# Adapter and mixture-of-experts block: six batches' results are summed among the dynamic expert blocks instead of at the end

## The chip, the cores and the metric

The kernel runs on one core of one Trainium2 chip. The metric is the device time of one execution in microseconds (us). TensorE is called PE here, its weight loads PEld, VectorE is DVE, ScalarE is ACT, GpSimd is POOL and SyncE, which issues most transfers, is SP.

## The reference

For 16 batches of 256 tokens of width D = 256 the reference computes an adapter chosen per batch, and a feed-forward block with one shared MLP and the best two of eight experts per token:

```python
# adapter: weights of the batch's profile
z = relu(x @ Wd + bd)                        # 256 -> 128
y = x + z @ Wu + bu                          # 128 -> 256
h = layernorm(y) * g + b
# feed-forward on h
router_probs = softmax(h @ gate_w + gate_b)  # 8 experts
expert_values, expert_indices = top_k(router_probs, k=2)
expert_values = expert_values / (sum(expert_values) + 1e-09)
moe_out = sum over the two experts e of value_e * (gelu(h @ ew1[e] + eb1[e]) @ ew2[e] + eb2[e])
shared  = gelu(h @ sh_w1 + sh_b1) @ sh_w2 + sh_b2      # 256 -> 1024 -> 256
return x + h + shared + moe_out
```

All of it is float32. How many tokens go to which expert is known only on the chip. For these inputs the experts get 940, 931, 1119, 1065, 1411, 1083, 845 and 798 of the 8192 pairs of token and expert.

## The kernel before, in words

**Numbers.** Weights and activations of the MLPs are split into two float16 parts, and a product is three matmuls (high by high, high by low, low by high). One *unit* is 256 tokens through one MLP: eight groups of six matmuls for the first product (`mm1`, L667) and eight for the second (`mm2`, L703). After each group of the first, ACT applies gelu (L674); after every fourth, the four results are split into high and low parts: high by ACT (L682) or DVE (L684), low by DVE (L688). A *half unit* has 128 tokens. The groups of one unit's first product alternate with those of the second product of the unit before (`unit_steps`); a second product that has not yet run waits in `pend`.

**Static stage, up to about 392 us.** A planner (`Plan`) is given operations with engine, duration, dependencies and a due time, and lays them out one after the other on all engines: of the operations that can start, it takes the one with the smallest key of start, due time and load. The constants `P_V`, `PACE` and `VE2` set due times: of the expert weights' preparation and of the units that fill PE. In this stage lie the adapter (L823, L839, L843), the transposes (L958), the gate (L977), the ranks of each token within its experts (L1047 to L1054), the scatter of each token's row into the experts' slots `xslot` in DRAM (L1092), 13 of the 16 shared units, the preparation of each expert's weights (squares on ACT at L533, high parts on ACT at L616, low parts on DVE at L622), the table of blocks, and the first 14 expert units. Each expert has two *static* blocks of 256 slots. Tokens of rank 512 and above belong to blocks whose expert is found on the chip.

**Dynamic stage, units s = 14 to 36.** Two static units are left (14, 15), then sixteen dynamic full units (16, 17, 18, 20 to 22, 24 to 26, 28 to 30, 32 to 34, 36) with half units between them (19, 23, 27, 31, 35). Here SP's and POOL's orders are as written in the code; PE, DVE and ACT are ordered by the framework's scheduler. In each unit SP issues the transposing loads of the rows of unit s+2 and their row numbers (`next_T`: L1227 and L1231, twice for a full unit), then its weights if the expert changes (`block_weights`: L1544, L1546), then for s = 19 to 34 one batch of x again (`x_again`, L1635). DVE takes a finished result from PSUM with its weights' scale and the bias (`take`, L1234), POOL scatters it to `yrow` in DRAM, where each token has two rows (`scatter_y`, L1240), and adds x and the shared bias into `base` for one batch (`add_x`, L1640, L1641).

**Weights of the two experts.** `top2_weights`, called in the loop at s = 18, takes Exp of the logits (L1580) and some thirteen small DVE operations; the scheduler puts it at 184 us, since it depends on the routing only.

**End.** The number of used blocks is read (L1672) and a branch (L1673) runs further half units if there are more than five; for these inputs there are not. Then shared unit 13 (`whole_unit`), eight loads of 1 MB of `yrow` into the buffers of the weights and of the adapter's result (`combine_load`, L1604), shared units 14 and 15, and for each of 16 batches `combine` and `store`. `combine` adds two rows times two weights into `base`: four operations on DVE (L1619) or, for even batches, two on DVE, two scales on ACT (L1617) and one add on POOL (L1624). Shared results are added into `base` by DVE (L1503).

## Time and profile before

| what | value |
|---|---|
| median of three runs | 665.37 us |
| lowest and highest | 664.24 and 669.65 us |
| the profiled execution | 666.21 us, span 664.4 us, granted clock 0.960 |
| PE busy | 614.1 us, 92% of the span |
| DVE, ACT, POOL busy | 410.4, 392.4, 242.1 us |
| chain that ended last | PE 75%, DVE 8%, DMA 6%, issue 5%, ACT 3% |
| moved by DMA | 131.57 MB |

The span is what the profiler sees from the first to the last instruction; the execution's own time is 1.8 us longer. A stretch of the profile gives, for each engine, the busy time and the number of instructions in it, the TensorE clock that was granted, and the share of time that the 16 DMA engines were busy. In a group of instructions the numbers behind the bar are busy time and mean duration, and behind the next bar the engine's idle time before them with what ended it. "PEq" and the like are the engines' sequencers; "issue" is time in which an engine waited for nothing that the profile shows.

### The profile page before, as it was taken

Reading aid. Unit: us, or ns where it says so; the run is one execution under the profiler, and the core shown is the slowest. Engines: PE = TensorE matmul, PEld = TensorE weight load, DVE = VectorE, ACT = ScalarE, POOL = GpSimd, SP = SyncE. Lnnn points to the kernel's source line nnn. Section 1 sums busy time; section 2 is a strip of 40 time slices with the busy share of each in tenths; the row PEclk is TensorE's granted clock in tenths of the full one; section 3 lists DMA queues with packets and bytes.
Section 4 is the critical chain, followed back from the end, with each engine's and each line's share of the span. In section 5 each row is a group of like instructions: output and inputs, shape, how many; then the busy total and the mean of one; then the engine's idle time right before and its main releaser. Section 6 shows DMA issues by size and latency. Waiting matters only on the chain.

```text
span 664.4 us, 15240 instructions
## 1 busy us (share of the span) xinstructions
PE 614.1 (92%) x5541; PEld 522.8 (79%) x5541; DVE 410.4 (62%) x980; ACT 392.4 (59%) x615; POOL 242.1 (36%) x370
## 2 busy tenths in 40 slices
PE   4699997999998899999999999999999999997962
PEld 3368785877887688888888888898989989896851
DVE  5678786988884263567665744444555546552498
ACT  1378575696794487888988744444444545442570
POOL 1003463356368201323212222333654655561132
PEclk8579998999999899999999999999999999998997
DMA  7784545925522249498799559828996599910496
GB/s 264 249 266 131 177 152 176 343 98 206 185 75 88 73 151 178 128 255 255 205 250 292 176 136 361 204 72 229 306 231 193 153 317 171 333 58 6 171 387 219
DMA packets 92570, 131.57 MB, mean 198 GB/s; under 512 B 53548, under 2 KB 69958, under 8 KB 84551
## 3 DMA queue, kind: packets, MB, share of 16 engines
q1 hardware_dynamic: 84914, 109.94, 56.9%
q0 software_dynamic: 6768, 18.43, 8.4%
q10 hardware_dynamic: 804, 2.16, 0.9%
q8 instruction: 45, 0.74, 0.5%
q14 instruction: 39, 0.31, 0.1%
HBM read 96.46 MB, written 41.28 MB: 207 GB/s over the span
## 4 chain that ended last, share of the span: by engine, by line
PE 75%; DVE 8%; DMA 6%; issue 5%; ACT 3%; POOL 1%; SPq 0%; DVEq 0%; POOLq 0%; ACTq 0%
PE bank L667 35%; PE bank L703 32%; DVE base L1619 4%; DMA yrow<-late,idt 3%; PE bank L839 3%; PE bank L823 3%; DMA wst<-in_adp_dram 1%; PE bank L958 1%; DVE hh L688 1%; PE bank L843 1%; ACT h L674 1%; PE bank L977 1%; DMA wst<-yrow 1%; DMA xslot<-late,sli 1%; ACT wst L616 1%
## 5 line engine op out<-in xcount | busy, mean ns | idle before, releaser
L703 PEld LDWEIGHTS <-hh 128*128 128x128 f16 x2424 | 234.1, 99 | 47.0 <-DVE hh L688 9.6
L674 ACT ACTIVATE h<-bank,tst 128x256 f32<-128x256 f32 x256 | 139.7, 561 | 120.8 <-PE bank L667 103.3
L703 PE MATMUL bank<-wst,hh 128*128 128x256 f16 x1536 | 208.9, 273 | 1.2 <-DVEq L1673 0.9
L667 PE MATMUL bank<-late,wst 128*128 128x256 f16 x1536 | 203.8, 273 | 0.8 <-ACT h L674 0.7
L1240 POOL DMA_INDIRECT yrow<-late,idt x69 | 90.0, 1304 | 256.0 <-DVE late L1234 195.6
L667 PEld LDWEIGHTS <-wst 128*128 128x128 f16 x1536 | 150.3, 98 | 18.5 <-issue 1.1
L703 PE MATMUL bank<-wsh,hh 128*128 128x256 f16 x768 | 107.8, 278 | 12.1 <-DVE hh L688 7.0
L667 PE MATMUL bank<-xlnT,wsh 128*128 128x256 f16 x768 | 108.3, 280 | 6.9 <-PEq L1673 3.1
L674 ACT ACTIVATE h<-bank,tsh 128x256 f32<-128x256 f32 x128 | 68.9, 559 | 65.7 <-PE bank L667 57.0
L684 DVE TENSOR_SCALAR hh<-h,tst 128x1024 f16<-128x1024 f32 x46 | 41.8, 909 | 92.7 <-ACT h L674 92.6
L667 PEld LDWEIGHTS <-wsh 128*128 128x128 f16 x768 | 75.7, 101 | 23.0 <-issue 10.6
L688 DVE SCALAR_TENSOR_TENSOR hh<-h,tst,hh 128x1024 f16<-128x1024 f32 x64 | 82.0, 1281 | 17.0 <-ACT hh L682 16.0
L1092 POOL DMA_INDIRECT xslot<-late,sli x64 | 69.8, 1091 | 50.6 <-issue 23.8
L688 DVE SCALAR_TENSOR_TENSOR hh<-h,tsh,hh 128x1024 f16<-128x1024 f32 x32 | 40.9, 1278 | 34.8 <-ACT hh L682 34.4
L1234 DVE SCALAR_TENSOR_TENSOR late<-bank,tst 128x256 f32<-128x256 f32 x64 | 30.7, 480 | 36.8 <-PE bank L703 30.8
L682 ACT ACTIVATE hh<-h,tsh 128x1024 f16<-128x1024 f32 x32 | 36.7, 1147 | 0.8
L1081 POOL IOTA late<- 128x32 int32 x32 | 4.8, 160 | 74.7 <-PE bank L958 40.6
L674 ACT ACTIVATE h<-bank,late 128x128 f32<-128x128 f32 x40 | 18.3, 457 | 20.8 <-PE bank L667 19.2
L622 DVE SCALAR_TENSOR_TENSOR wst<-wf,prep,wst 128x1024 f16<-128x1024 f32 x20 | 25.3, 1279 | 0.1
L839 PE MATMUL bank<-wst,zT 128*128 128x256 f32 x64 | 23.2, 447 | 0.3
L823 PE MATMUL bank<-xlnT,wst 128*128 128x256 f32 x64 | 20.4, 449 | 2.9 <-DMA wst<-in_adp_dram 2.8
L616 ACT ACTIVATE wst<-wf,prep 128x1024 f16<-128x1024 f32 x20 | 21.3, 1136 | 1.8 <-DVE prep L578 1.8
(225 smaller groups left out, 587.8 us busy)
## 6 DMA issues: line engine op xcount, KB each, us to landing
wst<-scr SPq DMA_DIRECT2D x32, 1024.0 KB
scr<-wst SPq DMA_DIRECT2D x16, 1024.0 KB
wf<-scr SPq DMA_DIRECT2D x10, 1024.0 KB
wst<-yrow SPq DMA_DIRECT2D x6, 1024.0 KB
wf<-in_ew_dram SPq DMA_DIRECT2D x5, 1028.0 KB
wf<-in_ew_dram SPq DMA_DIRECT2D x5, 1024.0 KB
wst<-in_adp_dram SPq DMA_DIRECT2D x16, 256.5 KB
xlnT<-in_xT_dram SPq DMA_DIRECT2D x16, 256.0 KB
```

The lines of the kernel that those rows point to most:

```text
L616: ACT.activation(self.w[:, a:b], self.wf[h][:, f], AF.Copy, scale=sc[:, 2 * h : 2 * h + 1],)
L667: mm = PE.matmul(pa[:, 0:n_tok], w1[:, wl, c, k, :], xin[:, xl, k, 0:n_tok], start=i == 0, stop=i == len(seq) - 1,)
L674: ACT.activation(h32[:, c % 4, 0:n_tok], pa[:, 0:n_tok], AF.Gelu_apprx_tanh, bias=tail[:, c : c + 1], scale=tail[:, 8:9],)
L682: ACT.activation(hi, h4, AF.Copy, scale=tail[:, 9:10])
L684: V.tensor_scalar(hi, h4, tail[:, 9:10], None, ALU.mult)
L688: V.scalar_tensor_tensor(hh[:, 1, c, 0:n_tok], h32[:, :, 0:n_tok], tail[:, 9:10], hh[:, 0, c, 0:n_tok], ALU.mult, ALU.subtract,)
L703: PE.matmul(py, hh[:, hl, k, t * P : (t + 1) * P], w2[:, wl, k, :], start=q == 0 and i == 0, stop=q == 3 and i == len(seq) - 1,)
L823: PE.matmul(pt_of(("z", b))[:, 0:S], wa()[:, k * P : (k + 1) * P], xf32(b)[:, k, :], start=k == 0, stop=k == KC - 1,)
L839: PE.matmul(pt_of(("y", b))[:, t * D : (t + 1) * D], zT()[:, t * P : (t + 1) * P], wa()[:, 256:512], start=True, stop=False,)
L1092: ins = POOL.indirect_dma_start(out=xslot[:, :], out_offset=bass.IndirectOffsetOnAxis(ap=sli[:, c, j : j + 1], axis=0), in_=payb[plan.slot ...
L1234: V.scalar_tensor_tensor(ysb, py, tail[:, 10:11], tail[:, 11 : 11 + D], ALU.mult, ALU.add)
L1240: ins = POOL.indirect_dma_start(out=yrow[:, :], out_offset=bass.IndirectOffsetOnAxis(ap=idt[:, t, :].bitcast(I32), axis=0), in_=ysb, in_of ...
```

## The change

1. `top2_weights` becomes part of the plan: its operations are given to the planner after the static units, and its first depends on the routing and on the result of static unit 11. The weights get one array, `wts`, and for the first six batches a second one, `wlate`, holds the weights of rows whose rank in their expert is 512 or more; in `wts` these are zero.
2. Six transfers write zeros to the rows of `yrow` that belong to the first six batches, in the planned stage.
3. The table gets a second count of tokens per expert, over the first six batches only, and `used` a second column: the number of used blocks, plus 64 if any of these counts is above 512.
4. In the dynamic loop, at the end of units 21 to 26, SP issues `y_load` of one of the batches 0 to 5 (512 KB); one unit later the batch is combined and stored. There are two buffers for these loads, in the adapter result's array.
5. `settle(9)` ahead of the branch goes; shared unit 13 is put ahead of it. The branch reads both columns, and is taken if the second is above the sure number; then the late rows of the six batches would be loaded, added and stored again. With these inputs the largest count of the first six batches is 475.
6. At the end five loads of 1 MB bring the other ten batches, which are combined and stored as before.
7. `P_V`, `PACE` and `VE2` get other values.

```diff
--- before.py
+++ after.py
@@ -34,6 +34,8 @@
 NHALF = 24
 SURE = 5
 TOP_AT = 18
+EARLY = 6
+EARLY_AT = TOP_AT + 3
 POS_F = 2 * NSTAT * E
 POS_H = POS_F + 2 * NFULL
 NPOS = POS_H + NHALF
@@ -145,9 +147,9 @@
         return out
 
 
-P_V = (82.0, 121.0)
-PACE = (0.0, 9.6, 24.7, 16.4)
-VE2 = 8.9
+P_V = (131.0, 214.35)
+PACE = (0.0, 8.17, 16.14, 17.464)
+VE2 = 11.504
 
 
 @with_exitstack
@@ -355,7 +357,7 @@
 
     metaf = const([1, 2, NFULL], I32, "metaf")
     metah = const([1, NHALF], I32, "metah")
-    used = const([P, 1], I32, "used")
+    used = const([P, 2], I32, "used")
     rowt = const([1, NPOS], I32, "rowt")
     PAD = NULLB
     pos = const([P, 1], F32, "pos")
@@ -1119,9 +1121,13 @@
             return const(shape, dt, "bt_" + name)
 
         pc = lambda: pt_of("count")[:, 0:E]
+        pc2 = lambda: pt_of("count")[:, E : 2 * E]
         cnt = plan.op(
             "PE", 0.2,
-            lambda: PE.matmul(pc(), ones, mc[:, NG, :], start=True, stop=True), 0.0,
+            lambda: (
+                PE.matmul(pc(), ones, mc[:, NG, :], start=True, stop=True),
+                PE.matmul(pc2(), ones, mc[:, EARLY // 2, :], start=True, stop=True),
+            ), 0.0,
             [mc_of[NG - 1]], acq=[("pt", "count")], lat=0.2,
         )
         nh, nhf = rt([P, E], I32, "nh"), rt([P, E], F32, "nhf")
@@ -1132,6 +1138,7 @@
         odd0, starts = rt([P, 1], F32, "odd0"), rt([P, 2, E], F32, "starts")
         sel, row = rt([P, 2, E], F32, "sel"), rt([P, 1], F32, "row")
         ei, prev = rt([1, P], I32, "ei"), rt([1, NFULL], I32, "prev")
+        over = rt([P, 1], F32, "over")
 
         pad = plan.op(
             "DVE", 0.1, lambda: V.tensor_tensor(padi, pc(), padbase, ALU.add), 0.0, [cnt]
@@ -1150,6 +1157,7 @@
 
             pads.append(plan.op("POOL", 1.36, pad_scatter, A(NB) + 2, [pad, *last], land=P * PW * 2))
         fns = [
+            lambda: V.tensor_reduce(over, pc2(), AX.X, ALU.max),
             lambda: V.tensor_scalar(nh, pc(), float(P - 1), None, ALU.add),
             lambda: V.tensor_scalar(nh, nh, 7, None, ALU.logical_shift_right),
             lambda: V.tensor_copy(nhf, nh),
@@ -1209,7 +1217,9 @@
                 V.memset(prev[:, i : i + 1], E - 3 + r)
             V.tensor_tensor(metaf[:, 1, :], metaf[:, 0, :], prev, ALU.not_equal)
             V.tensor_scalar(metah, ei[:, POS_H:NPOS], E - 1, None, ALU.min)
-            V.tensor_copy(used, ends[:, 1, E - 1 : E])
+            V.tensor_scalar(over, over, float(NSTAT * BLK), 64.0, ALU.is_gt, ALU.mult)
+            V.tensor_copy(used[:, 0:1], ends[:, 1, E - 1 : E])
+            V.tensor_scalar(used[:, 1:2], over, ends[:, 1, E - 1 : E], None, ALU.add)
 
         plan.op("DVE", 1.0, meta, 300.0, [got])
         plan.op("DVE", 0.1, lambda: V.memset(spot, 0.0), 0.0, [got, o], add=["pa", "py0", "py1"])
@@ -1398,6 +1408,53 @@
         for s in range(NSTAT * e, min(NSTAT * e + NSTAT, NPLAN)):
             static_unit(s)
 
+
+
+    wts = const([P, 2, NTILE], F32, "wts")
+    wlate = const([P, 2, 2 * EARLY], F32, "wlate")
+
+    def top2_weights(v):
+        T8 = [P, NTILE, E]
+        rs, den = const([P, NTILE], F32, "rs"), const([P, NTILE], F32, "den")
+        rk, beyond = const([P, 2, 2 * EARLY], I32, "rk"), const([P, 2, 2 * EARLY], F32, "beyond")
+        tmp, ex = [z.rearrange("p (j e) -> p j e", e=E) for z in ztb]
+        o = plan.op(
+            "DVE", 0.4,
+            lambda: V.tensor_tensor(tmp, L, m1.unsqueeze(2).broadcast_to(T8), ALU.subtract),
+            v, [*gate_of.values(), sli_of[NG - 1], *ydone.values(), ev_last[NPLAN - 3]],
+        )
+        o = plan.op("ACT", 3.0, lambda: ACT.activation(ex, tmp, AF.Exp), v, [o])
+        fns = [lambda: V.tensor_reduce(rs, ex, AX.X, ALU.add), lambda: V.reciprocal(rs, rs)]
+        for c in range(2):
+            fns += [
+                lambda c=c: V.tensor_tensor(tmp, ex, oh[:, c], ALU.mult),
+                lambda c=c: V.tensor_reduce(wts[:, c, :], tmp, AX.X, ALU.add),
+                lambda c=c: V.tensor_tensor(wts[:, c, :], wts[:, c, :], rs, ALU.mult),
+            ]
+        e2 = slice(0, 2 * EARLY)
+        fns += [
+            lambda: V.tensor_tensor(den, wts[:, 0, :], wts[:, 1, :], ALU.add),
+            lambda: V.tensor_scalar(den, den, 1e-9, None, ALU.add),
+            lambda: V.reciprocal(den, den),
+            lambda: V.tensor_tensor(
+                wts, wts, den.unsqueeze(1).broadcast_to([P, 2, NTILE]), ALU.mult
+            ),
+            lambda: V.tensor_scalar(rk, sli[:, :, e2], EBLK * P - 1, None, ALU.bitwise_and),
+            lambda: V.tensor_scalar(beyond, rk, float(NSTAT * BLK), None, ALU.is_ge),
+            lambda: V.tensor_tensor(wlate, wts[:, :, e2], beyond, ALU.mult),
+            lambda: V.tensor_tensor(wts[:, :, e2], wts[:, :, e2], wlate, ALU.subtract),
+        ]
+        return tiny(fns, v, [o], dur=0.22, first=0.4)
+
+    top2_weights(0.0)
+    for b in range(EARLY):
+        plan.op(
+            "SP", 0.5,
+            lambda b=b: SP.dma_start(
+                yrow[2 * b * S : 2 * (b + 1) * S, :].rearrange("(p k) d -> p k d", p=P),
+                padrow[:, 0 : 2 * D].bitcast(F32).unsqueeze(1).broadcast_to([P, 4, D]),
+            ), 60.0 + 12 * b, after=[z_of[b + 8]], land=P * 4096,
+        )
     ahead_T = {}
     for s in (NPLAN, NPLAN + 1):
         u = units[s]
@@ -1565,63 +1622,30 @@
             g2(c)
         settle(9)
 
-    w1t = const([P, NTILE], F32, "w1t")
-    w2t = const([P, NTILE], F32, "w2t")
-    cp = ctx.enter_context(tc.tile_pool(name="cp", bufs=1))
-
-    def top2_weights():
-        T8 = [P, NTILE, E]
-
-        def rt(shape, name):
-            return cp.tile(shape, F32, tag=name, name=name)
-
-        tmp, ex = [z.rearrange("p (j e) -> p j e", e=E) for z in ztb]
-        V.tensor_tensor(tmp, L, m1.unsqueeze(2).broadcast_to(T8), ALU.subtract)
-        ACT.activation(ex, tmp, AF.Exp)
-        rs = rt([P, NTILE], "rs")
-        V.tensor_reduce(rs, ex, AX.X, ALU.add)
-        V.reciprocal(rs, rs)
-        pv = rt([P, 2, NTILE], "pv")
-        for c in range(2):
-            V.tensor_tensor(tmp, ex, oh[:, c], ALU.mult)
-            V.tensor_reduce(pv[:, c, :], tmp, AX.X, ALU.add)
-            V.tensor_tensor(pv[:, c, :], pv[:, c, :], rs, ALU.mult)
-        den = rt([P, NTILE], "den")
-        V.tensor_tensor(den, pv[:, 0, :], pv[:, 1, :], ALU.add)
-        V.tensor_scalar(den, den, 1e-9, None, ALU.add)
-        V.reciprocal(den, den)
-        V.tensor_tensor(w1t, pv[:, 0, :], den, ALU.mult)
-        V.tensor_tensor(w2t, pv[:, 1, :], den, ALU.mult)
-
-    def combine_load(g):
-        if g < NBUF:
-            yl = wst[g]
-        else:
-            yl = xlnT[:, 0:8].rearrange("p b l k s -> p (b l k s)")
-        yl = yl.bitcast(F32).rearrange("p (j c d) -> p j c d", c=2, d=D)
-        for h in range(2):
-            r0 = 2 * (g * TG + h * TG // 2)
-            SP.dma_start(
-                yl[:, 4 * h : 4 * h + 4].rearrange("p j c d -> p j (c d)"),
-                yrow[r0 : r0 + TG, :].rearrange("(j p c) d -> p j (c d)", p=P, c=2),
-            )
+    def y_load(yl, t0, nt):
+        SP.dma_start(
+            yl.rearrange("p j c d -> p j (c d)"),
+            yrow[2 * P * t0 : 2 * P * (t0 + nt), :].rearrange("(j p c) d -> p j (c d)", p=P, c=2),
+        )
         return yl
 
-    def combine(b, yl):
-        j0 = 2 * b % (TG // P)
+    def y_view(flat, nt):
+        return flat.bitcast(F32).rearrange("p (j c d) -> p j c d", c=2, d=D)[:, 0:nt]
+
+    def combine(b, yl, w=wts, lean=False):
         for t in range(2):
             j = 2 * b + t
-            for c, w in ((0, w1t), (1, w2t)):
-                y = yl[:, j0 + t, c, :]
-                if c == 1 and b in POOLED:
-                    ACT.activation(y, y, AF.Copy, scale=w[:, j : j + 1])
+            for c in range(2):
+                y = yl[:, t, c, :]
+                if c == 1 and b in POOLED and not lean:
+                    ACT.activation(y, y, AF.Copy, scale=w[:, c, j : j + 1])
                 else:
                     V.scalar_tensor_tensor(
-                        base[:, j, :], y, w[:, j : j + 1], base[:, j, :], ALU.mult, ALU.add
+                        base[:, j, :], y, w[:, c, j : j + 1], base[:, j, :], ALU.mult, ALU.add
                     )
-        if b in POOLED:
+        if b in POOLED and not lean:
             bb = base[:, 2 * b : 2 * b + 2, :]
-            POOL.tensor_tensor(bb, bb, yl[:, j0 : j0 + 2, 1, :], ALU.add)
+            POOL.tensor_tensor(bb, bb, yl[:, :, 1, :], ALU.add)
 
     def store(b):
         SP.dma_start(
@@ -1647,8 +1671,11 @@
     u = units[NPLAN - 1]
     u["ids"] = idb[plan.slot["id", NPLAN - 1]]
     ET = mybir.EngineType
+    flat = xlnT.rearrange("p b l k s -> p (b l k s)")
+    early_buf = [y_view(flat[:, o * 1024 : (o + 2) * 1024], 2) for o in (4, 6)]
     with tc.manual_schedule(engines={ET.SP, ET.Pool}):
         xr = None
+        early = {}
         pend.append((g2_steps(hhb[hh_turn], views(u["w"])[1], evac_of(u), 2), 2))
         for s in range(NPLAN, NU):
             u = units[s]
@@ -1659,31 +1686,46 @@
                 block_weights(units[s + 2])
             if s in HLOAD:
                 block_weights(HLOAD[s])
-            if s == TOP_AT:
-                top2_weights()
             if xr is not None:
                 add_x(s - TOP_AT - 2, xr)
                 xr = None
             if TOP_AT < s <= TOP_AT + NB:
                 xr = x_again(s - TOP_AT - 1)
+            b = s - EARLY_AT - 1
+            if b in early:
+                combine(b, early[b])
+                store(b)
+            b = s - EARLY_AT
+            if 0 <= b < EARLY:
+                early[b] = y_load(early_buf[b % 2], 2 * b, 2)
         if xr is not None:
             add_x(NB - 1, xr)
-        settle(9)
-        count = nc.values_load(used[0:1, 0:1], min_val=0, max_val=2 * NFULL + NHALF)
-        with tc.If(count > 2 * NFULL + SURE):
-            for j in range(SURE, SURE + 2):
-                extra_half(j)
-            with tc.If(count > 2 * NFULL + SURE + 2):
-                for j in range(SURE + 2, NHALF):
+        whole_unit()
+        most = 2 * NFULL + NHALF
+        count = nc.values_load(used[0:1, 0:1], min_val=0, max_val=most)
+        any_left = nc.values_load(used[0:1, 1:2], min_val=0, max_val=most + 64)
+        with tc.If(any_left > 2 * NFULL + SURE):
+            with tc.If(count > 2 * NFULL + SURE):
+                for j in range(SURE, SURE + 2):
                     extra_half(j)
-        whole_unit()
-        yl = {g: combine_load(g) for g in range(NT // TG)}
+                with tc.If(count > 2 * NFULL + SURE + 2):
+                    for j in range(SURE + 2, NHALF):
+                        extra_half(j)
+            for b in range(EARLY):
+                combine(b, y_load(early_buf[b % 2], 2 * b, 2), wlate, lean=True)
+                store(b)
+        yl = {}
+        for i, b in enumerate(range(EARLY, NB, 2)):
+            space = flat[:, 0:8192] if i < 2 else wst[(i - 2) // 2]
+            h = i % 2 * 4096
+            v = y_load(y_view(space[:, h : h + 4096], 4), 2 * b, 4)
+            yl[b], yl[b + 1] = v[:, 0:2], v[:, 2:4]
         for _ in fillers:
             pass
-        for b in range(NB - 1):
-            combine(b, yl[b * S // TG])
+        for b in range(EARLY, NB - 1):
+            combine(b, yl[b])
             store(b)
-        combine(NB - 1, yl[NT // TG - 1])
+        combine(NB - 1, yl[NB - 1])
         flush()
         store(NB - 1)
 
```

## The prediction

> **What bounds the kernel now.** I read the busy time by stretch first, then the chain that ended last, then the queue of SyncE (SP). Columns: stretch, its length, busy time of PE, PEld, DVE, ACT, POOL (with counts), granted clock, DMA share, GB/s.
>
> ```profile
> core 0: us, PE busy (x) PEld busy (x) DVE busy (x) ACT busy (x) POOL busy (x), PEclk, DMA share, GB/s
> 99.70:116.30 16.60, 13.19 (x83) 8.88 (x83) 10.07 (x34) 8.72 (x13) 5.25 (x12) 0.90 0.53 175
> 182.00:232.00 50.00, 43.99 (x389) 35.41 (x388) 24.21 (x101) 31.40 (x47) 28.93 (x52) 0.97 0.23 76
> 232.00:598.00 366.00, 364.77 (x3460) 327.69 (x3458) 204.03 (x287) 222.24 (x361) 134.87 (x163) 1.00 0.78 212
> 598.00:664.40 66.40, 44.35 (x365) 36.52 (x362) 42.10 (x67) 27.83 (x50) 15.09 (x15) 0.88 0.55 196
> ```
>
> PE sets the time from 232 to 598 us (1.23 us idle). So only three things can move the end: 22.1 us of idle PE in the tail, about 9.4 us in the two earlier stretches (3.4 and 6.0), and any stall put into the full middle. The tail, from the chain, PE's timeline and SP's:
>
> ```profile
> 607.93 1.44 PE L667 MATMUL bank<-xlnT,wsh 128*128 128x256 f16 x6 [3.14 <-PEq L1673]
> 618.79 3.94 DMA yrow<-late,idt
> 622.75 5.09 DMA wst<-yrow
> 650.69 9.42 DVE base L1619 x17
> 622.75 7.09 SPq L1604 DMA_DIRECT2D wst<-yrow  x6
> ```
>
> The branch costs PE 3.14 us; the last scatter lands 3.94 us after its issue, the first 1 MB load 5.09 us after that; then VectorE (DVE) combines without a pause until 661.2 and the store ends the span at 664.4, 3.2 us later. PE's last matmul is at 653.3. The tail is bound by a late start and by 16 batches of combining.
>
> **Tail: what is removed.** Six of 16 combines leave it, and shared unit 13 goes ahead of the branch. In the instruction order PE now has 220 matmuls behind the branch instead of 312. Groups of six take 0.655 us in the chain, so one matmul is 0.109 us. Before the branch PE starts the last dynamic unit's second product at 600.9 and has 116 matmuls from there: 12.7, so 613.6. (Interleaving the shared unit also covers the 0.91 us that PE waited on DVE there.) The branch costs 3.1 to 3.6 again: 617. Then 24.0 of matmuls and about 1 of slow clock: PE could end at 642.
>
> The loads wait for the last scatter. Its product ends after 96 of those matmuls, 611.4; take and scatter issue add 0.8, landing 3.94, POOL's join with the branch 0.85 (its semaphore instruction at L1673): loads at about 617, first data at 622 by the 5.09 row. The DVE rows of this tail:
>
> ```profile
> L1619 DVE SCALAR_TENSOR_TENSOR base<-wst,w1t,base 128x256 f32<-128x256 f32 x24 | 16.1, 717 | 3.0 <-DMA wst<-yrow 3.0
> L1624 POOL TENSOR_TENSOR base<-base,wst 128x512 f32<-128x512 f32 x6 | 8.1, 1350 | 24.7 <-DVE base L1619 11.6 <-ACT h L674 9.6 <-DMA out_dram<-base 3.6
> ```
>
> DVE runs from 628.3 to 661.2. Of these 32.9 us four splits L688 take 1.2 each in the chain, six L1503 0.4 each and pauses 1.5; the remaining 24.2 are eight pairs of batches, 3.0 a pair. With five pairs and the rest unchanged: 15.1 + 4.8 + 2.4 + 1.5 = 23.8, from 622 to 645.8. The last split stands behind the combines in DVE's order; 24 matmuls (2.6), one take (0.5) and the store (3.2) follow: about 652.1 against 664.4. **Tail: −12**; bounds −18 (the end set by PE: 642 and the same store and take) and −8 (data 4 us later: one more landing of a scatter in the way).
>
> **Dynamic stage: what is added.** Each of six batches adds to SP a load of 512 KB (y_load) at the end of unit b+21 and a store of 256 KB one unit later; to DVE four or two L1619 operations at 0.47; to ScalarE (ACT) two scales at 0.50 for even batches; to POOL one add at 1.35. The engine work, 1.9 us a unit, lies beside PE: from 232 to 598 DVE is busy 56%, ACT 61%, POOL 37%. What matters are waits on in-order queues. SP, POOL and the DMA share before:
>
> ```profile
> 463.98 1.23 SPq L1227 DMA_TRANSPOSE late<-xslot  x1
> 470.53 2.07 SPq L1546 DMA_DIRECT2D wst<-scr  x2
> 474.46 1.25 SPq L1227 DMA_TRANSPOSE late<-xslot  x1
> 481.23 1.38 SPq L1546 DMA_DIRECT2D wst<-scr  x2
> 466.07 1.77 POOL L1240 DMA_INDIRECT yrow<-late,idt  x1 [2.17 <-DVE late L1234]
> 479.69 1.35 POOL L1641 TENSOR_TENSOR base<-base,sb_b 128x512 f32<-128x512 f32 x1
> 454.00:480.00 26.00, 26.00 (x257) 23.48 (x255) 13.89 (x17) 11.43 (x22) 14.53 (x15) 1.00 1.07 319
> ```
>
> The reader sees two transposes with weights behind them (units 24 and 25, which PE begins at 483.0 and 491), unit 20's second scatter, a POOL add, and a DMA that is already full. Batch 0's load cannot go before that scatter has landed: 466.07 + 3.94 = 470.0. Unit 24's transpose stood at 463.98 and is queued behind it, so its weights go at about 477.5 instead of 470.5; landing in 5.09 they meet 483.0 just in time. The slack of some 7 us is spent. Then store 0 waits for POOL's new add, which follows the add ending at 481.04: 482.4. Batch 1's load goes at 482.9, unit 25's transpose at 484, its weights at 491 instead of 481.2 and land at 496 where PE wants them at 491: a stall of 3 to 5, say 4. DVE has the combine in the middle of a unit, ahead of its next splits, and waits there for the load to land; the scatters of that unit wait for the same landing. Half units (23, 27) are shortest: 2 to 6 us of DVE wait each, of which I let 1.25 reach PE in each of four units: 5. Later weights (unit 30): 1. **Dynamic stage: +10.** A 512 KB load's landing isn't in the trace: the 256 KB store's 3.2 from below, 1 MB's 5.09 from above; I take 5.09, since the stretch is full. Bounds: +3 (landing 3.2, only the stall of unit 25) and +19 (each of four waits costs PE 3.5).
>
> The Trainium skill, "SBUF — State Buffer", section "The DMA setup-cost knee", fits 2 us plus bytes at 436 GB/s to one transfer. An estimate from it is 3.2 us for 512 KB and 4.4 for 1 MB, where this trace has 5.09 for 1 MB; by it the stage would cost nearer +5 than +10.
>
> The same page, section "SBUF: two separate sides", says that a DVE operation with two SBUF inputs and a GpSimd operation that reads SBUF exclude each other for the whole instruction. The trace agrees: L1619 takes 0.47 alone and up to 1.49 beside POOL's 1.35. It speaks against putting combines among POOL's adds: up to 1.0 us more on each of two operations a unit. By the row that is 2 us a unit of DVE, beside 44% idle; by the rule, if each falls on a split that PE waits for, 6 units × 2 = 12 more.
>
> **Static stage: what is moved.** The weights' softmax leaves the routing stage for the planner, behind static unit 11, and new constants of pace reorder preparation and routing.
>
> ```profile
> 184.56 1.28 ACT L1580 ACT_TABLE_LOAD   x1
> 185.86 0.42 ACT L1580 ACTIVATE zT<-zT 128x256 f32<-128x256 f32 x1
> ```
>
> This Exp and the load back to gelu (1.28 at 187.33) are 2.98 us of ACT on the chain there. Behind unit 11 they lie where ACT has 39% idle; with that cover gone they would cost the same 3. Thirteen small DVE operations move along, four new ones come: 17 × 0.2 = 3.4 us, under DVE's idle 44%. Preparation of expert 0 (an ACT piece of 4.26 us at 101.43) now comes after most routing and no longer cuts into it. Of the 9.4 us idle I credit the 3.0 of Exp and about half of the remaining 6.4: **−6**. Bounds −12 (that and clock lost in these stretches) and +6 (routing, pulled tighter, starves PE twice as much as now). Six zero writes of 512 KB cost SP six issues of about 0.5 where the DMA share is 0.57: 0 to +1. The table's second count matmul and three more small DVE operations add less than 1 us beside the routing.
>
> **Sum.** −12 + 10 − 6 = −8. The profiled execution took 666.21 with a span of 664.4, and lies 0.84 above the median of 665.37; −8 from the median gives **657.4**. Within 1% (658.7 to 672.0) is what a measurement here can hardly tell from no change.
>
> **Rivals.**
> 1. *Early batches hidden.* Loads land in 3.2, stalls stay at +3: −12 + 3 − 6 = −15, **650**. For it: weights asked for two units ahead and 44% idle DVE. Against it: the slack of 7 us that one late scatter uses up.
> 2. *The wait moves.* The tail's gain returns as stalls of +19: −12 + 19 − 6 = +1, **666.4**. For it: SP is one queue with the transposes behind each y_load, and already waited 24.2 us for PE at L1227. Against: those waits are slack.
> 3. *DMA becomes the bound* (slower). Places: units 21 to 28, share 1.07 already. Six times 768 KB is 4.6 MB, at some 288 GB/s 16 us of a full DMA; with the waits' +10 that is +26: −12 + 26 − 6 = +8, **673.4**. It decides once the stage costs more than 12 + 6 + 6.7 = 24.7. Against it: from 506 to 598 the share is 0.72, so part of the debt is repaid.
> 4. *Routing starves* (slower): static +6 instead of −6, with 14 in the dynamic stage: −12 + 14 + 6 = +8, **673.4**. Against it: PE is idle least where shared units fill in, and they still do.
> 5. *The branch is taken*, and six batches are combined again: at least 6 × 3 = 18 us more. Counting the inputs' routes, no expert has more than 475 tokens in the first six batches, below the 512 of two static blocks. Excluded.
>
> **Chances.** Forecast 0.38 (own range 651 to 663: 0.27 faster, 0.11 within 1%); rival 1 0.21; rival 2 0.17; rival 3 0.18; rival 4 0.06. So faster 0.48, same 0.28, slower 0.24. The range of 643 to 675 takes in rivals 1 to 4 and leaves out most of their outer bounds: 0.05 below, 0.14 above.
>
> **What would show it.** Right: behind the branch some 24 us of matmuls, five 1 MB loads and ten combines, the end about 35 us behind their issue; first stalls of PE in the dynamic stage at units 25 to 28, released by weights or DVE's split; the stretch 182 to 232 with under 3 us of idle PE. Wrong: a dynamic stage without idle PE (then 650), a DMA share near 1 through unit 30 with PE waiting for transposes (then 673), or a routing stage that ends later than 232.

## The result, and the profile after

The changed kernel takes 698.15 us (median of four runs, 692.7 to 703.38) where the kernel before takes 664.81 beside it: a ratio of 1.046, with a 95% interval of 1.037 to 1.055. The forecast was 657.4, faster; it is slower by 33 us.

Two anchors split both traces into three parts: the first gelu of unit 14 and that of unit 36. The execution profiled first, 703.38 us, is the slowest of the four, so the lines below are of a second profile of the same kernel (run after_again), on a chip where the kernel before takes 645.38 us and this one 676.07, a ratio of 1.047 (1.042 to 1.051).

| part | before | first profile after | second profile after | forecast |
|---|---|---|---|---|
| start to unit 14 (static) | 388.3 | 399.5 | 371.4 | −6 |
| unit 14 to unit 36 (dynamic) | 205.7 | 237.1 | 238.7 | +10 |
| unit 36 to the end (tail) | 70.4 | 65.0 | 65.6 | −12 |

The static part differs from chip to chip; the other two hardly do. The kernel before was not profiled on the second chip. An estimate from its time there is 645.4 − 1.8 − 205.7 − 70.4 = 367.5 us for its static part, against 370.0 for the changed kernel by the same sum (676.1 − 1.8 − 238.7 − 65.6) and 371.4 in its profile: the change costs 2 to 4 us there. On the first chip the other three spans (690.9 to 696.5) less 238 and 65 leave 388 to 393, that is 0 to +5. The loss is in the dynamic stage: +31 to +33.

The busy times by stretch, second profile: units 14 to 21, units 22 to 30, units 31 to 35, tail. The second block is the whole dynamic stage of the kernel before.

```profile
core 0: us, PE busy (x) PEld busy (x) DVE busy (x) ACT busy (x) POOL busy (x), PEclk, DMA share, GB/s
371.40:448.70 77.30, 77.30 (x734) 69.55 (x733) 35.55 (x46) 35.19 (x64) 23.59 (x31) 1.00 0.74 210
448.70:565.10 116.40, 93.83 (x819) 79.30 (x817) 55.33 (x71) 39.92 (x79) 54.79 (x53) 0.91 0.67 206
565.10:610.10 45.00, 45.00 (x459) 40.85 (x457) 26.17 (x31) 20.91 (x41) 26.16 (x28) 1.00 0.81 215
610.10:675.70 65.60, 49.05 (x401) 40.65 (x399) 33.08 (x51) 27.58 (x48) 15.39 (x14) 0.92 0.37 130
```

```profile
388.30:594.00 205.70, 205.70 (x2004) 185.76 (x2002) 107.59 (x127) 94.76 (x177) 95.51 (x108) 1.00 0.80 220
```

Ahead of unit 22 and after unit 30 PE is as full as before. Between them, where the six batches are loaded, summed and stored, it is idle for 22.6 us, and its granted clock is 0.91 over 116.4 us, worth about 10 us more: together the 33 us. The DMA share of 0.67 says that the DMA engines are not full on the mean of this stretch. Who waited in this stretch (total, times, longest):

```profile
DVE base L1643 <- DMA xlnT<-yrow: 39.2, 6, 9.6
POOL yrow L1250 <- DVE late L1244: 37.3, 12, 11.1
ACT xlnT L1641 <- DMA xlnT<-yrow: 24.2, 3, 11.1
...
ACT h L676 <- DVE hh L690: 13.1, 3, 6.4
...
PE bank L669 <- ACT h L676: 8.6, 3, 5.4
...
PE bank L705 <- DVE hh L686: 6.0, 3, 3.9
...
PE bank L669 <- DMA wst<-scr: 5.4, 3, 2.5
...
PE bank L705 <- DVE hh L690: 2.5, 3, 1.2
```

And on SP's queue, before the early loads (L1626) and the stores (L1651):

```profile
SPq L1626 <- DMA yrow<-late,idt: 22.0, 4, 9.7
SPq L1651 <- POOL spot L1249: 16.4, 3, 7.5
```

DVE stands in every one of the six combines (L1643) for its load, and ACT in the scales (L1641) of the three even batches. POOL's scatters wait for DVE's takes (L1244), which stand behind the combines. PE then waits 17.1 us for gelu and splits that are queued behind combines, and 5.4 us for weights. One turn of it, from the timeline:

```profile
461.69 1.00 POOL L1250 DMA_INDIRECT yrow<-late,idt  x1 [7.79 <-DVE hh L686]
...
462.99 1.20 POOL L1250 DMA_INDIRECT yrow<-late,idt  x1 [0.19 <-DVE hh L690]
...
466.80 1.27 POOL L1648 TENSOR_TENSOR base<-base,xlnT 128x512 f32<-128x512 f32 x1
...
468.09 0.40 SPq L1651 DMA_DIRECT2D out_dram<-base  x1
...
470.51 0.37 SPq L1626 DMA_DIRECT2D xlnT<-yrow  x1
...
471.68 1.22 SPq L1237 DMA_TRANSPOSE late<-xslot  x1
...
474.96 1.67 DVE L1643 SCALAR_TENSOR_TENSOR base<-xlnT,wts,base 128x256 f32<-128x256 f32 x4 [9.63 <-DMA xlnT<-yrow]
...
475.70 1.01 POOL L1250 DMA_INDIRECT yrow<-late,idt  x1 [7.60 <-DMA late<-xslot]
...
477.08 0.39 PE L705 MATMUL bank<-wf,hh 128*128 128x256 f16 x2 [3.94 <-DVE hh L686]
...
478.30 1.35 SPq L1603 DMA_DIRECT2D wst<-scr  x2
...
484.52 1.46 PE L669 MATMUL bank<-late,wst 128*128 128x256 f16 x6 [2.54 <-DMA wst<-scr]
```

Read it downwards. Two scatters; POOL's add for batch 0 behind them; the store that waits for the add; batch 1's load behind the store and the landing of the second scatter, 7.5 us after its issue; DVE stands 9.63 us for that load; the next scatter goes out only after the load has landed (the profile puts its wait down to a transposing load issued behind that load); PE stands 3.94 us for the split behind the combine. The transposes (471.68) and weights (478.30) behind the load are late too, and PE waits for the weights at 484.52. It is a ring: load, combine, split, product, result, scatter, store, load.

The tail is shorter by 5 us, not 12. PE's timeline behind the branch:

```profile
634.90 1.44 PE L669 MATMUL bank<-xlnT,wsh 128*128 128x256 f16 x6 [3.89 <-PEq L1707]
636.13 1.48 PE L705 MATMUL bank<-wsh,hh 128*128 128x256 f16 x6
637.41 1.00 PE L669 MATMUL bank<-xlnT,wsh 128*128 128x256 f16 x6
638.25 0.27 PE L705 MATMUL bank<-wsh,hh 128*128 128x256 f16 x1
642.10 1.22 PE L705 MATMUL bank<-wsh,hh 128*128 128x256 f16 x5 [3.58 <-issue]
643.12 4.04 PE L669 MATMUL bank<-xlnT,wsh 128*128 128x256 f16 x18
```

Nineteen matmuls after the branch PE stops for 3.58 us with nothing to wait for, in the middle of a group of six, and the 18 behind that group take 4.04 us. DVE's first combine starts with the first data, and then DVE stands for a split that needs PE's products:

```profile
638.75 1.67 DVE L1643 SCALAR_TENSOR_TENSOR base<-xlnT,wts,base 128x256 f32<-128x256 f32 x4 [8.62 <-DMA xlnT<-yrow]
648.02 1.28 DVE L690 SCALAR_TENSOR_TENSOR hh<-h,tsh,hh 128x1024 f16<-128x1024 f32 x1 [7.60 <-ACT hh L684]
```

### The profile page after: what moved, and what is told of

Its sections match the earlier page's. It is cut to its first block, busy times and chain, and to the rows that moved or that the text cites. A ratio compares the mean times of both kernels' runs of the same rounds, so it can differ in the third digit from the quotient of the medians.

```text
span 701.6 us, 15276 instructions
## 1 busy us (share of the span) xinstructions
PE 627.7 (89%) x5542; PEld 531.0 (76%) x5542; DVE 412.7 (59%) x987; ACT 389.1 (55%) x614; POOL 246.6 (35%) x370
## 5 line engine op out<-in xcount | busy, mean ns | idle before, releaser
L705 PEld LDWEIGHTS <-hh 128*128 128x128 f16 x2424 | 238.2, 100 | 63.3 <-DVE hh L690 13.5
L669 PE MATMUL bank<-late,wst 128*128 128x256 f16 x1536 | 208.0, 276 | 8.7 <-DMA wst<-scr 5.0
L1250 POOL DMA_INDIRECT yrow<-late,idt x69 | 85.9, 1245 | 279.1 <-DVE late L1244 241.6
L705 PE MATMUL bank<-wsh,hh 128*128 128x256 f16 x768 | 112.6, 287 | 16.6 <-DVE hh L690 6.6
L690 DVE SCALAR_TENSOR_TENSOR hh<-h,tst,hh 128x1024 f16<-128x1024 f32 x64 | 86.6, 1353 | 19.3 <-ACT hh L684 18.5
L1094 POOL DMA_INDIRECT xslot<-late,sli x64 | 71.8, 1122 | 72.5 <-issue 33.8
L669 PEld LDWEIGHTS <-wsh 128*128 128x128 f16 x768 | 77.5, 103 | 21.5 <-issue 8.5
L1643 DVE SCALAR_TENSOR_TENSOR base<-xlnT,wts,base 128x256 f32<-128x256 f32 x30 | 14.7, 540 | 47.3 <-DMA xlnT<-yrow 47.3
L1244 DVE SCALAR_TENSOR_TENSOR late<-bank,tst 128x256 f32<-128x256 f32 x64 | 30.4, 478 | 18.3 <-PE bank L705 16.6
L669 PE MATMUL bank<-late,wf 128*128 128x128 f16 x240 | 20.6, 224 | 5.5 <-ACT h L676 5.5
L1324 DVE SCALAR_TENSOR_TENSOR base<-bank,tsh,base 128x256 f32<-128x256 f32 x26 | 12.5, 481 | 20.4 <-PE bank L705 12.6
```

The lines of the kernel that those rows point to most:

```text
L669: mm = PE.matmul(pa[:, 0:n_tok], w1[:, wl, c, k, :], xin[:, xl, k, 0:n_tok], start=i == 0, stop=i == len(seq) - 1,)
L690: V.scalar_tensor_tensor(hh[:, 1, c, 0:n_tok], h32[:, :, 0:n_tok], tail[:, 9:10], hh[:, 0, c, 0:n_tok], ALU.mult, ALU.subtract,)
L705: PE.matmul(py, hh[:, hl, k, t * P : (t + 1) * P], w2[:, wl, k, :], start=q == 0 and i == 0, stop=q == 3 and i == len(seq) - 1,)
L1094: ins = POOL.indirect_dma_start(out=xslot[:, :], out_offset=bass.IndirectOffsetOnAxis(ap=sli[:, c, j : j + 1], axis=0), in_=payb[plan.slot ...
L1244: V.scalar_tensor_tensor(ysb, py, tail[:, 10:11], tail[:, 11 : 11 + D], ALU.mult, ALU.add)
L1250: ins = POOL.indirect_dma_start(out=yrow[:, :], out_offset=bass.IndirectOffsetOnAxis(ap=idt[:, t, :].bitcast(I32), axis=0), in_=ysb, in_of ...
```

## The experiments

Ratios are to the kernel before, run beside each kernel on the same chip. "Stage" is the dynamic part, from the profile, 205.7 us before.

**Static stage.** Edits: the three constants of before put into the changed kernel (old_pace), the three new ones into the kernel before (new_pace).

```diff
-P_V = (82.0, 121.0)
-PACE = (0.0, 9.6, 24.7, 16.4)
-VE2 = 8.9
+P_V = (131.0, 214.35)
+PACE = (0.0, 8.17, 16.14, 17.464)
+VE2 = 11.504
```

> The changed kernel with the three constants of before (P_V, PACE, VE2). Theory S, the new order of the static stage costs what the traces show (unit 14 begins at 399.5 us instead of 388.3): about 11 us less than the changed kernel's 698, so 687, and unit 14 begins near 388. Rival T, the planned softmax and the zero writes cost it, not the constants: unit 14 stays near 399 and the time near 698. Both leave the dynamic stage (units 14 to 36) at about 237 us, against 205.7 before.

> The kernel before with the three new constants alone. Theory S: unit 14 begins about 11 us later, 676 in all. Rival T: unit 14 near 388 and 665. By the prediction's own term for the reordering it would be faster, about 661.

old_pace: 1.052 (1.045 to 1.060), unit 14 at 404.6 us, stage 238.7. new_pace: 1.0125 (1.007 to 1.018), unit 14 at 403.1, stage 206.0. On the same chip unit 14 is at 396.1 with the constants and softmax of before (run shared_ahead) and at 392.9 with the new constants and the planned softmax (run load_first). So each half alone costs 7 to 8.5 us in these profiles (one of each), and both together cost nothing there (−3): theory S fails for the pair, and T as well. The new constants belong to the planned softmax; that the two together gain over the kernel before is not shown.

**Shared unit ahead of the branch, alone.**

```diff
-        settle(9)
+        whole_unit()
         count = nc.values_load(used[0:1, 0:1], ...)
...
-        whole_unit()
         yl = {g: combine_load(g) for g in range(NT // TG)}
```

> The kernel before with shared unit 13 put ahead of the branch alone. By the prediction's tail the loads of results are issued at about 617 instead of 622.75 us and DVE combines all 16 batches without a pause after them: 5 to 6 us less, about 659.5. Rival: the branch costs more with the two units' work piled up ahead of it (5.3 us of idle PE in the changed kernel, 3.1 before), and what is gained ahead of it is lost again: 663 to 665.

Ratio 1.0007 (0.998 to 1.003), tail 72.3 against 70.4: the expected 5 to 6 us did not come. PE's timeline there:

```profile
626.24 1.44 PE L667 MATMUL bank<-xlnT,wsh 128*128 128x256 f16 x6 [3.53 <-PEq L1673]
...
632.83 0.80 PE L703 MATMUL bank<-wsh,hh 128*128 128x256 f16 x3 [2.70 <-issue]
633.42 3.42 PE L667 MATMUL bank<-xlnT,wsh 128*128 128x256 f16 x18
```

The branch costs 3.53, about as before (3.14), but the same pause without a cause follows, 2.70 us, with slow matmuls behind it. In the kernel before, where the result loads start nearly 15 us after PE has passed the branch, there is none. So the rival came true, nothing gained; but the branch itself grew by 0.4 us only, and the pause is the larger part of what is lost.

**Load at the unit's start.** The `y_load` block moved from the end of the loop's body ahead of `unit_steps`.

> The changed kernel with each y_load issued at the start of its unit instead of its end, so that it waits for a scatter one unit older. Theory W, the dynamic stage's extra 31 us are the loop from a scatter's landing through y_load, DVE's combine, the splits behind it and the next scatter: the DVE waits for the loads (38.8 us) nearly vanish, the stage falls by 15 to 25 us, to 675 to 683. Rival B, the DMA engines' bytes are what is short (share near 1, 4.6 MB more): the stage keeps at least 25 of its 31 us, 692 or more.

Ratio 1.0445 (1.037 to 1.052), stage 245.9: a clear miss. In the code's order the last scatter ahead of the start of unit s is that of unit s−2, and the load waits for it all the same, now ahead of both transposes: the first load goes out at 467.05 us, 8 us after PE has begun unit 21. The framework put the combine earlier too. DVE still stands 37.8 us at its loads. The experiment did not remove the wait that it was to remove.

**The changed kernel again, and parts left out.**

```diff
 # resident, no_load
+    resident = [y_view(flat[:, o * 1024 : (o + 2) * 1024], 2) for o in (8, 10)]
-                combine(b, early[b])
+                combine(b, resident[b % 2])
 # no_load, in addition
-                early[b] = y_load(early_buf[b % 2], 2 * b, 2)
+                early[b] = None
 # loads_only
-            if b in early:
-                combine(b, early[b])
-                store(b)
```

> The changed kernel unchanged, beside the runs below on their chip: ratio near 1.046 to the kernel before. The dynamic stage, from the first gelu of unit 14 to that of unit 36, is expected to be 235 to 240 us again (205.7 before) if its loss belongs to the order of the work; if it was an accident of one execution it is below 225.

> The changed kernel, but the early combines read two buffers that nothing loads, while the six loads are still issued as they were (the six batches' expert sums are left out of the result). Theory W, the in-order waits of DVE and ACT for the landing of the loads: PE's stalls released by splits and gelu go, the dynamic stage falls from about 237 to 215 or less, the time by 20 or more against the changed kernel. Rival Q, SP's queue: the load's wait for the scatter and the store's wait for POOL hold back transposes and weights behind them: the stage stays above 225, with PE waiting for wst<-scr. Rival B, bytes: also above 225.

> As the run with resident buffers, and the six early loads aren't issued either (the six batches' expert sums are left out); combines and stores stay. What it gains beyond that run is the price of the loads on SP's queue and on the DMA engines. Theory W: at most 5 us more, stage 206 to 215. Rival Q: the load's half of it, 10 to 15 more; what stays above 206 belongs to the stores.

> The changed kernel with its six early loads, but without the six combines and stores (the six batches are left out of the result). Theory W: nobody waits for the loads but SP and the scatters behind them, so the stage is 206 to 215. Rival Q: the load's wait alone holds SP up by 7 us a unit as the prediction had for batch 0, 215 to 225. Rival B: the bytes are there still, above 220.

Stages 238.7, 227.5, 219.8 and 225.5; ratios 1.047, 1.034, 1.020 and 1.0235 (intervals within 0.006 of these). Taking away the wait for the loads gives back 11 us, not 20; the loads alone, with nobody summing, cost 20; combines and stores without any load cost 14. Theory W missed in all three runs. Q held for the first, missed loads_only by half a microsecond, and expected 10 to 15 us between resident and no_load where there are 8. B held in the two runs for which it gave a number, so these runs don't exclude it; the plain loads below do. In loads_only PE's waits in the stretch of the early loads (440 to 565 us) are one line:

```profile
PE bank L669 <- DMA wst<-scr: 13.5, 3, 7.4
```

Every part of the early work stalls PE by itself, and by different ways. The loads do it through SP's queue, where they wait 26.3 us for scatters. In no_load PE waits 6.0 us for weights, which stand behind stores that wait 17.1 us for POOL, and 3.9 us for gelu; the combines there wait 25.0 us for POOL.

**Order on DVE and ACT, order on SP, both; and the loads of the tail held back.**

```diff
 # by_hand, behind_T_hand
-    with tc.manual_schedule(engines={ET.SP, ET.Pool}):
+    with tc.manual_schedule(engines={ET.SP, ET.Pool, ET.DVE, ET.Activation}):
...  (the tail keeps the former order)
 # behind_T, behind_T_hand: at n == 6, behind next_T, for units 21 to 28
+                    if units[s + 2]["nt"] == 2:
+                        block_weights(units[s + 2])
+                    if b >= 2:
+                        store(b - 2)
+                    if b < EARLY:
+                        early[b] = y_load(early_buf[b % 2], 2 * b, 2)
 # hold_loads
         yl = {}
+        next(fillers)
+        SP.dma_start(pos, h32b[st["h"]][:, 0, 0:1])
```

> The changed kernel with DVE's and ACT's order in the dynamic loop as written in the code, so that a combine stands behind its unit's splits and takes instead of in the middle of it; SP's order as it was. Theory W (a third of the loss, 11 of 33 us, as the run with resident buffers shows): stage 225 to 230 instead of 238.7, PE still waits for wst<-scr. If the rest were W too, 215 or less. If the place in DVE's order does not matter, 236 to 240. Units 14 to 21, which have no combine, are the control: 10.5 us a full unit.

> The changed kernel with SP's order altered in the loop: the transposes and the weights of unit s+2 are issued first, then a store of two units before, then y_load; combine as it was. Theory Q, two thirds of the loss are transposes and weights held up behind y_load's wait for a scatter and the store's wait for POOL: PE's waits for wst<-scr go and the stage falls to 215 to 222. If DVE's waits alone make the loss, it stays above 232.

> Both edits, SP's order and DVE's and ACT's. Theories W and Q together: stage 206 to 212, close to the 205.7 of before, and a ratio near 1.00 to 1.01 to the kernel before, since the tail is some 5 us shorter and the static stage some 4 longer. Theory B (bytes) would keep it above 218.

> The changed kernel with the five loads at the end held back until the first gelu after the branch, by one small transfer that reads its result. Theory F, the 3.6 us in which PE stands 19 matmuls behind the branch with nothing to wait for are the fetch of its next instructions behind the loads' bytes: the pause falls below 1 us, and the tail (unit 36 to the end) from 65.6 to about 61, though the loads come some 3.5 us later. Rival: the pause belongs to the branch and stays; tail 65 to 69.

Stages: by_hand 235.3, behind_T 229.5, behind_T_hand 225.9. All three are above what theories W and Q said, and the last lies where B would have kept it; two orders together give back 13 of 33 us of the stage. Ratios: by_hand 1.033 (1.028 to 1.039), behind_T_hand 1.032 (1.026 to 1.0385); behind_T has medians of 690.26 and 665.40 without an interval. In behind_T_hand ACT still stands 11.1 us at one load, the scatters wait 14.6 us for early loads, and the stores wait 19.3 us for POOL (16.4 in the changed kernel); only the loads' wait for scatters fell, from 22.0 to 6.8.

hold_loads did what theory F says. Its ratio, 1.041 (1.033 to 1.048), does not stand clear of the changed kernel's 1.046, but in the profile the tail is 62.2 instead of 65.6, and PE runs through:

```profile
656.07 1.44 PE L669 MATMUL bank<-xlnT,wsh 128*128 128x256 f16 x6 [3.79 <-PEq L1707]
...
659.47 0.82 PE L705 MATMUL bank<-wsh,hh 128*128 128x256 f16 x6
660.13 2.13 PE L669 MATMUL bank<-xlnT,wsh 128*128 128x256 f16 x18
```

The pause is gone though the loads come later, and 18 matmuls take 2.13 us instead of 4.04. The trace's packets on the instruction queue agree: the second 16 KB packet behind the branch starts 3.2 us after the first in hold_loads (653.46 and 656.64), 3.3 us in the kernel before, 7.0 in shared_ahead and 7.6 in the changed kernel, where 1 MB loads were issued in between. The other profiles say the same: the pause is there, 1.8 to 3.6 us after 18 to 21 matmuls, in all 16 profiles in which the loads are issued at the branch, and in none of the four in which they are issued later. That the packet's lateness is queueing behind the loads' bytes is the reading that fits them; the queue itself is not seen.

**What keeps the last 20 us.** Plain loads of the same rows in place of the transposing ones, and on them the three edits.

```diff
 # all plain kernels
-            SP.dma_start_transpose(
-                out=xgT[:, :, :, t * P : (t + 1) * P].rearrange("p l k s -> p (l k) s"),
-                in_=src[:, 0 : 2 * D],
-            )
+            SP.dma_start(
+                xgT[:, :, :, t * P : (t + 1) * P].rearrange("p l k s -> p (l k) s"),
+                src[:, 0 : 2 * D].rearrange("p (a s) -> p a s", s=P),
+            )
 # plain_free_...: scatters of units from 16 on and the early loads
+            apart("early", ins)
```

> The kernel before with plain loads of the same rows in place of the transposing loads (the experts get rows that are not transposed: this part is left out). PE sets the dynamic stage in the kernel before, so all theories expect 205 to 206 us from unit 14 to unit 36 and a ratio within 0.99 to 1.01. It is the base for the three runs beside it.

> The changed kernel with plain loads in place of the transposing ones (transposition left out). Theory B, transposing loads and bytes keep the DMA engines full and make loads and weights land late: the stage falls from 238.7 to 225 or less. Theory L, the lock between early loads and scatters, and P, the store behind POOL: 230 to 238.

> As plain_after, and the early loads and the scatters of units from 16 on are declared independent (the rows that count in the loads are not written by those units). Theory L: SP's waits at y_load for scatters and POOL's for loads vanish, and the stage is 10 to 18 us below that of plain_after, at 220 or less. Theories B and P: within 4 us of plain_after.

> As plain_free_loads, with transposes' plain loads and weights ahead of store and y_load on SP, and DVE's and ACT's order as written, combines at the unit's end. Theories L and P together: 206 to 211, and a time within 1% of plain_before's. If something else holds the stage, above 215.

> As plain_free_T_hand (205.9 us from unit 14 to unit 36), with the dependency between early loads and scatters put back; plain loads, so transposition is left out. If the lock between them is what left 20 us in the run behind_T_hand (225.9): 218 to 226. If the transposing loads were: 206 to 212.

> As plain_free_T_hand, with DVE's and ACT's order left to the framework again, so that combines stand in the middle of units; plain loads, so transposition is left out. If the place of the combine matters once SP and POOL no longer wait: 212 to 222, with DVE's and ACT's waits for xlnT<-yrow back. If it matters only together with the lock: 206 to 210.

| kernel | SP's order | DVE's and ACT's order | load and scatters | stage | PE idle in it |
|---|---|---|---|---|---|
| plain_before | – | – | – | 205.7 | 0 |
| plain_after | old | framework | wait for each other | 234.7 | 20.9 |
| plain_free_loads | old | framework | free | 228.5 | 16.1 |
| plain_T_hand | new | written | wait for each other | 220.2 | 9.7 |
| plain_free_T | new | framework | free | 216.2 | 7.8 |
| plain_free_T_hand | new | written | free | 205.9 | 0 |

Ratios: plain_before 0.998 (0.995 to 1.002), plain_after 1.030 (1.021 to 1.039), plain_free_loads 1.031 (1.019 to 1.043), plain_free_T_hand 0.998 (0.994 to 1.002), plain_free_T 1.0195 (1.008 to 1.031); plain_T_hand has medians of 683.58 and 673.62 without an interval.

Theory B falls: without transposing loads the stage loses 4 us, where some 14 or more were expected. (The ratio fell by more, to 1.030; by the profiles the rest lies in the tail and the static part.) L alone gives 6 in the stage, short of the expected 10 to 18, and nothing in the time. But put back alone into the version with all three edits, the lock costs 14 us, and the combine's place in the middle of units 10. The 14 rest on one profile, of an execution of 689.53 us; the other execution of plain_T_hand took 677.62, 4 us above the kernel before, so the size of the lock's price is uncertain. The 10 are in line with the ratio of 1.0195. In the run with the lock put back POOL is seen in it, where the free one has no such line:

```profile
POOL yrow L1250 <- DMA xlnT<-yrow: 14.5, 3, 7.0
```

and in the run with the framework's order DVE and ACT stand at the loads again:

```profile
DVE base L1649 <- DMA xlnT<-yrow: 17.6, 4, 6.2
ACT xlnT L1647 <- DMA xlnT<-yrow: 14.9, 3, 5.5
```

With all three edits the stage is that of the kernel before, with the same early transfers and the same 18 early operations on DVE, 6 on ACT and 3 on POOL:

```profile
387.80:593.70 205.90, 205.90 (x2006) 185.93 (x2005) 128.01 (x145) 97.45 (x182) 86.98 (x111) 1.00 0.73 242
```

So with plain loads the cause is shown: the ring, held at several places at once; neither the bytes nor the engines' work cost anything there. For the changed kernel itself, with transposing loads, it is inferred: there is no result with the free dependency. The old order on SP was not put back alone. That the rows of loads and scatters do not meet is argued from the ranks (at most 475 of 512 in the six batches); no run here shows it in a result. And the ceiling is seen: even with a free dynamic stage and a tail of 64.1 us, the time is within the interval of the kernel before. No version here beats it.

## Why the prediction was wrong

1. **What bounds the kernel** was read rightly: PE full in the dynamic stage, gains only in the tail and in the early idle time, and "any stall put into the full middle" as the danger.
2. **The dynamic stage's term, +10, is the step that failed**; +33 is outside its bounds of +3 to +19. Its mechanism was there: y_load behind the scatter, the store behind POOL's add, transposes and weights behind both, DVE ahead of its splits. Of the +33, PE waited 17.1 us for gelu and splits, 5.4 for weights, and some 10 were lost by its clock; the sum had 5, 5 and nothing. Three sizes failed.
   - "I let 1.25 reach PE in each of four units: 5." PE was idle 17.1 us for gelu and splits. The number had no row behind it. DVE's 39.2 us of waiting are six waits of 2.6 to 9.6, where four of 2 to 6 were taken; nearly half got through, since splits stand behind the combine and gelu behind the splits. ACT's own wait for the same loads, 24.2 us in the scales of the even batches, is not in the sum at all, and gelu stands behind it too.
   - The waits were added up as if each were met by an undisturbed kernel. In fact a late load delays the scatters, which delay the store and the next load: a ring with a period longer than a unit. Batch 1 already saw a load that came out of batch 0's delay. A scatter's landing, taken as 3.94, was 7.5 there. A unit of 7.9 us took 23.5 (unit 24), one of 10.1 took 19.4 (unit 26), from first gelu to first gelu.
   - The clock was left out: 10 us. Around the end of each of five stalls of 2.0 to 5.4 us PE's clock went to half for 3.4 us, with the longest for twice that; half of these 20 us is the loss:

```profile
477.40:480.70 3.30, 2.64 (x14) 1.83 (x14) 3.27 (x4) 1.02 (x2) 2.91 (x3) 0.50 0.61 126
484.20:487.50 3.30, 2.98 (x15) 2.06 (x16) 0.00 (x0) 0.00 (x0) 0.00 (x0) 0.50 1.01 372
491.10:494.40 3.30, 2.64 (x13) 1.90 (x13) 2.34 (x4) 2.54 (x6) 0.78 (x1) 0.50 0.17 34
518.40:525.10 6.70, 5.00 (x33) 4.14 (x33) 3.62 (x6) 3.69 (x9) 3.80 (x4) 0.50 0.31 74
552.50:555.80 3.30, 3.30 (x17) 2.31 (x16) 0.27 (x1) 0.56 (x1) 1.12 (x1) 0.50 1.16 317
```

   The rule for it is in the Trainium skill, "TensorE: Matmul & The Clock Gate", section "Part 1: The HAM clock gate (the "warmup" mystery)": after an idle window of about 3.4 us the clock is at half, until a busy window of that length lets it up again. The trace agrees on the half and on the length. It also shows that the window ahead need not be idle throughout: from 480.90 to 484.10, ahead of the second line, PE was busy for 1.08 us. The prediction allowed 1 us of slow clock in the tail and none here.
3. **The weights' wait** was sized well: 3 to 5 us for unit 25 and 1 for unit 30, against 5.4 us measured in three waits, of 0.9, 2.5 and 2.0 us ahead of units 24, 25 and 30; the total fits better than its parts. The load's landing was taken as 5.09: from issue to the first operation that waited for it the six loads took 3.5 to 6.3 us, 4.3 on the mean (batch 1's 4.45, from 470.51 to 474.96). The 3.2 us estimated from the Trainium skill, "SBUF — State Buffer", section "The DMA setup-cost knee", is for a transfer alone, and all six measurements stand above it, three of them by less than 0.5 us.
4. **The tail, −12**, was −5. The loads went out and the first data came when the sum said, 23.0 and 28.6 us after unit 36's first gelu (forecast 23 and 28). What the sum lacked is DVE's 7.6 us in front of a split in the middle of the combines: the split needed products that PE's pause of 3.58 and the slow matmuls behind it held back. From there DVE worked to the last split almost without a pause, as forecast. The pause was not in the trace of before at all, where nothing was loading when PE passed the branch. The branch itself cost 3.9 (5.3 in the first profile, with a pause of 1.93) where 3.1 to 3.6 were taken. With loads held back the tail was −8.
5. **The static stage, −6**, was 0 to +5. That Exp leaves a busy place is true; that idle time there is therefore saved is not: the plan lays the work out anew, and the new constants alone cost 8 us. The sign that the prediction named, under 3 us of idle PE from 182 to 232, came in the second profile (none), not in the first (6.8, against 6.0 before), where PE is also idle for 8.8 us from 116 to 182 (1.0 before). Which operations make the difference was not taken apart.
6. **The rivals.** The one that came true, slower, was forecast through the DMA engines' bytes ("It decides once the stage costs more than 12 + 6 + 6.7 = 24.7."). The threshold was passed, but not by bytes: the share was 0.67 in the stretch, and with plain loads the stage without stalls had the same early transfers. The rival "the wait moves" had the right mechanism and stopped at +19. A forecast of slower needed a sum over a ring instead of over waits.
7. The shared port (the Trainium skill, "SBUF — State Buffer", section "SBUF: two separate sides") was weighed at up to 12 us more. In plain_free_T_hand a combine's operation still takes up to 2.02 us beside POOL's adds instead of 0.47, as the rule says, and the stage costs nothing: DVE is busy for 128.0 of its 205.9 us, and PE waits for none of it.

## What to carry to other kernels

Where work is put among full stages, draw its ring first: what it waits for, what is queued behind it on each in-order engine, and whether one of these releases what it waits for next; if the ring closes, the sum of single waits is too low a price. Price stalls of TensorE with their clock: here 22.6 us of them cost 10 more. Ask of each new wait on a shared DRAM tensor whether the rows really meet, and look whether a gain's ceiling, here 5 to 8 us of tail, pays for the risk.

## What the runs showed of the hardware

Behind a branch that was not taken TensorE can run out of work when data loads are issued just then: with 1 MB loads issued as PE passed the branch, PE stopped for 2.70 us (shared_ahead), 1.93 and 3.58 us (the changed kernel) in the middle of a group, and the second packet on the instruction queue came 7.0 us or more after the first; with the loads held back until one gelu later it came after 3.2 us and PE did not stop. That the fetch of instructions waits behind the data is the likely reading.
